# A graph network's second edge loop: penalty tables, paired outputs, and smaller macros at the end

## The chip, the cores and the metric

The kernel runs on one core of a Trainium2 chip. Its time is the device time of one execution in microseconds; the figure for a kernel is the median of its runs. One further execution is taken with the hardware profiler, and all views below come from that one. PE is the matrix engine (PEld its weight loads), DVE the vector engine, ACT the scalar engine, POOL the engine that issues the gathers here, SP the engine that issues the plain DMAs.

## What is computed

6250 nodes with 128 features, 100,000 edges sorted by destination, 64 features an edge. Two layers, each added to its input and normalised:

```python
# layer 0: messages, mean over the edges of a destination
m = relu(x[src] @ W_ne[:128] + (edge_attr @ W_edge) @ W_ne[128:] + b_ne)
out = segment_sum(m, dst) / max(count, 1) + x @ W_self + b_self
x = layernorm(x + out)
# layer 1: attention with 4 heads of 32, every node also has a loop to itself
xl, xr = x @ w_l + b_l, x @ w_r + b_r
logits = (leaky_relu(xl[src] + xr[dst], 0.2) * att).sum(-1)
ex = exp(logits - segment_max(logits, dst)[dst])
out = segment_sum(xl[src] * ex / segment_sum(ex, dst)[dst], dst) + bias
out = (out - out.mean()) / (out.std() + 1e-5) * ln_w + ln_b
x = layernorm(x + out)
```

## The kernel before

The edges are cut into 784 tiles of 128, four tiles a group: 196 groups of 512 edges. For every tile POOL issues one indirect DMA that gathers 128 rows of 128 features by source (`gather`, L251) into a ring of 30 group slots. The program first makes the node tables; then it has two loops over the 196 groups, written as steps in which every engine's instructions stand in a fixed order (a manual schedule):

- the first edge loop (layer 0; pool `e0`), gathers from `xw_t`;
- the second edge loop (layer 1; pool `e1`), gathers from `xl_t`;
- a short end (`n2`) for the normalisation over all nodes.

In step `s` of the second loop, the gather of group `s+4` is issued, SP stores the sums of the step before and loads rows for a later group (`load_rows`: a window of `xr_t` into `xr` and the destinations into `ds`), and then:

- `both` (L668, L670): PE adds the turned gathered rows and the destinations' rows in PSUM, group `s`;
- `copy_both` (ACT, L674) and `leaky` (DVE, L677) for group `s-1`; `logits` (PE, L696) for `s-2`;
- `onehot_t` (ACT, L661 and L662) for `s+1`;
- `sums` of the groups due in this step: four products (L825), and a last product (L831) with the row carried over from the group before, which DVE scales (`old`, L829). `keep_sums` copies the result (`win`, L836), and SP stores it to `out_t` at a row that it first loads from `fst` into a register (`store_sums`, L839);
- `values` (DVE, L816) and `onehot` (DVE, L454) for the groups due in the next step;
- whatever is planned for this step: the stages of a macro, and outputs.

A macro is the set of groups whose segment maxima are found together: 4 heads x 12 groups are 48 rows of 512 logits. Its ten stages, one per step, are `m_logits` (ACT copies the logits; DVE makes the penalties `pen`, which are -1e30 where the destination changes, L716 and L717), `m_forward` and `m_back` (a running maximum in each direction on DVE, L721 and L725), `m_ends` (PE turns the rows' ends, L736), `m_groups` (DVE, a scan over the groups), `m_before` (PE, L757), `m_maxima` (DVE; the penalty of the first segment `fp` at L766, the maxima at L768; then Exp on ACT), `m_weights` (DVE scales an identity, `dg`, L791; PE turns the weights, L780 and L795), `m_left` (DVE copies `cb`, L800; PE turns the rest) and `m_ready` (ACT). Groups of a macro can be summed from two steps after its last stage. There are 17 macros: fifteen of 12 groups, one of 9, one of 7.

```python
when, busy = {}, {}
begin = []
for k, m in enumerate(MS):
    begin.append(max(m.g0 + m.mg + 2, begin[k - 1] + 6 if k else 0))
    ...
    for u in range(m.g0, m.g0 + m.mg):
        s = max(begin[k] + len(M_STEPS) + 1, when.get(u - 1, 0))
        while busy.get(s, 0) >= (1 if s < GN - 30 else 2):
            s += 1
```

So sums go one a step, and two a step from step 166 on. A block of 128 nodes is finished when its last group is summed: `out_load` reads it from `out_t`, `out_weights` three steps later and `output` one more step later compute on DVE (L852 to L875, and L246 to L248). There are 49 blocks, of which the last two come together at the very end. Steps 0 to 195 take up a group each; the last step is 218.

Of the kernel before, what the change touches and what calls it, by code (L numbers as in the profile page):

```python
# [9 lines left out]
F32 = mybir.dt.float32  # L10
# [3 lines left out]
OP = mybir.AluOpType  # L14
# [3 lines left out]
P = 128  # L18
N = 6250
E = 100000  # L20
D = 128
DE = 64
H, C = 4, 32
SLOPE = 0.2
EPS = 1e-5
NB = -(-N // P)
# [28 lines left out]
RAW = 12  # L55
MACROS = (12,) * 15 + (9, 7)
AHEAD = 4
# [18 lines left out]
def gnn_resnorm(  # L76
# [353 lines left out]
    def near():  # L430
        ctx = ExitStack()
        with ctx:
            keep = ctx.enter_context(tc.tile_pool(name="near", bufs=1))
            sum_t = dram.tile([NR, W0], F32, name="sum_t")
            xr_t = dram.tile([NR, D], F32, name="xr_t")
            out_t = dram.tile([NR, H * HV], F32, name="out_t")
            kps = ctx.enter_context(tc.tile_pool(name="nearp", bufs=1, space=PSUM))
            rows_q = kps.tile([P, W + D], F32, name="rows_q")
# [7 lines left out]
            for t, n in ((sum_t, W0), (out_t, H * HV)):  # L446
                nc.scalar.dma_start(t[NP - P:NP, :], zero[:, 0:n])
                nc.scalar.dma_start(t[NP:NR, :], zero[:, 0:n])
            nc.scalar.dma_start(xr_t[NP:NR, :], zero[:, 0:D])

            def onehot(pool, g, dtype):
# [183 lines left out]
            with tc.tile_pool(name="e1", bufs=3) as pool, tc.tile_pool(name="e1m", bufs=2) as mp, \  # L635
# [14 lines left out]
                XR, DS, PZ, Z, OH, V, PA, WIN, OUTS = {}, {}, {}, {}, {}, {}, {}, {}, {}  # L650

                def load_rows(g):
                    XR[g] = pool.tile([W, D], F32, name="xr", bufs=9)
                    nc.sync.dma_start(XR[g], xr_t[bass.ds(first_row(g), W), :])
                    DS[g] = pool.tile([W, S], F32, name="ds", bufs=9)
                    nc.sync.dma_start(DS[g], bass.AP(tensor=dpad.tensor, offset=dpad.offset + 1 + g * S,
                                                     ap=[[0, W], [1, S]]))
# [14 lines left out]
                def copy_both(g):  # L672
                    Z[g] = pool.tile([P, S], F32, name="z")
                    nc.scalar.copy(Z[g], PZ[g])  # L674
# [27 lines left out]
                def m_load(m):  # L702
                    m.dm = mp.tile([m.R, S + 2], F32, name="dm")
                    for h in range(H):
                        nc.sync.dma_start(m.dm[h * m.mg:(h + 1) * m.mg, :],
                                          bass.AP(tensor=dpad.tensor, offset=dpad.offset + m.g0 * S,
                                                  ap=[[S, m.mg], [1, S + 2]]))

                def m_logits(m):
                    m.lg = mp.tile([m.R, S], F32, name="lg")
                    nc.scalar.copy(m.lg, m.plg)

                    m.pen = mp.tile([m.R, S + 1], F32, name="pen")
                    nc.vector.tensor_tensor(m.pen, m.dm[:, 1:], m.dm[:, 0:S + 1], op=OP.not_equal)  # L716
                    nc.vector.tensor_scalar(m.pen, m.pen, -BIG, None, op0=OP.mult)  # L717

# [4 lines left out]
                def m_back(m):  # L723
                    m.sm = mp.tile([m.R, S], F32, name="sm", bufs=1)
                    nc.vector.tensor_tensor_scan(m.sm[:, ::-1], m.pen[:, S:0:-1], m.fw[:, ::-1], -BIG,  # L725
                                                 op0=OP.add, op1=OP.max)

                    m.ends = mp.tile([m.R, 2], F32, name="ends")
                    nc.vector.tensor_scalar(m.ends[:, 0:1], m.dm[:, S:S + 1], m.dm[:, 0:1], -BIG,
                                            op0=OP.not_equal, op1=OP.mult)  # L730
                    nc.vector.tensor_copy(m.ends[:, 1:2], m.fw[:, S - 1:S])

                def m_ends(m):
                    m.pe = ps1.tile([P, S], F32, name="pw")
                    for i in range(2):
                        nc.tensor.transpose(m.pe[0:1, i * P:i * P + m.R], m.ends[:, i:i + 1], ident[0:m.R, 0:m.R])  # L736

# [22 lines left out]
                def m_maxima(m):  # L760
                    R = m.R
                    prev = mp.tile([R, 1], F32, name="prev")
                    nc.vector.tensor_copy(prev, m.pv[0:R, 0:1])

                    fp = mp.tile([R, S], F32, name="fp", bufs=1)
                    nc.vector.tensor_scalar(fp, m.dm[:, 1:S + 1], m.dm[:, 0:1], -BIG, op0=OP.not_equal, op1=OP.mult)  # L766
                    m.mx = mp.tile([R, S], F32, name="mx")
                    nc.vector.scalar_tensor_tensor(m.mx, fp, prev, m.sm, op0=OP.add, op1=OP.max)  # L768
# [65 lines left out]
                def keep_sums(u):  # L834
                    WIN[u] = pool.tile([W, H * HV], F32, name="win", bufs=4)
                    nc.scalar.copy(WIN[u], PA[u])  # L836

                def store_sums(u):
                    nc.sync.dma_start(out_t[bass.ds(first_row(u), W), :], WIN.pop(u))  # L839

# [48 lines left out]
                when, busy = {}, {}  # L889
                begin = []  # L890
                for k, m in enumerate(MS):
# [14 lines left out]
                stop = max(when.values())  # L906
                for b in range(NB - last):
                    s = when[FINAL[b]] + 1
                    for i, f in ((1, out_load), (4, out_weights), (5, output)):
                        plan(s + i, f, b, 1)  # L910
                    stop = max(stop, s + 5)
                stop += 1
# [9 lines left out]
                for s in range(stop + 1):  # L922
# [355 lines left out]
```

## Time and profile before

| | us |
|---|---|
| median of 3 runs | 2864.68 (2855.61 to 2869.66) |
| the profiled execution | 2204.19 |
| its span, first to last instruction | 2202.5 |
| mean granted TensorE clock | 0.83 |
| first gather from `xw_t`, last gather from `xw_t` issued | 83, 1000 |
| first gather from `xl_t`, last gather from `xl_t` issued | 1037, 2040 |
| PE, DVE, ACT, POOL busy | 1576, 1306, 715, 1508 |

The runs without the profiler are 660 us longer than the profiled execution. Busy shares are means over stages that have different limits; a stretch of the trace, or a single step, tells more. A row of the slices is 55 us wide, and a digit is the busy share in tenths.

### The profile page before, as it was taken

The numbers are of one execution on the slowest core, as the hardware profiler recorded it, in microseconds if no ns is written. First come the engines' busy times: TensorE is split into PE (matmuls) and PEld (weight loads), VectorE is DVE, ScalarE is ACT, GpSimd is POOL, SyncE is SP. The second block draws the span as 40 slices with busy tenths as digits, with TensorE's granted clock in tenths as the row PEclk, the third lists the DMA queues.
The fourth block names the chain that finished last, engine by engine and source line by source line (L and its number), as shares of the span: only waits on it lengthen the run. The fifth ranks groups of instructions, "written<-read, shape, count | busy, mean of one in ns | idle before, by whom it ended". The sixth has DMA issues, their size and how long they took to land.

```text
span 2202.5 us, 27258 instructions
## 1 busy us (share of the span) xinstructions
PE 1576.4 (72%) x6577; PEld 884.7 (40%) x6577; DVE 1306.1 (59%) x3710; ACT 715.0 (32%) x1724; POOL 1508.2 (68%) x1574
## 2 busy tenths in 40 slices
PE   4796566656666666674778888888888888889660
PEld 2574444444444444442223333333434344434440
DVE  4584445555666667775124455555556666677776
ACT  1341111111122112221344444444444444445214
POOL 7577777777777777772777777777777777777000
PEclk7897777777777787775779999999999999988755
DMA  5554444444444444432433444444444444443011
GB/s 148 143 119 96 95 95 95 93 99 99 99 98 103 105 103 101 106 90 80 119 101 105 112 113 115 114 113 111 112 113 116 115 113 119 111 115 101 24 26 59
DMA packets 292634, 225.37 MB, mean 102 GB/s; under 512 B 143289, under 2 KB 247591, under 8 KB 292466
## 3 DMA queue, kind: packets, MB, share of 16 engines
q1 hardware_dynamic: 241200, 120.47, 20.5%
q0 software_dynamic: 50048, 102.60, 19.9%
q8 instruction: 56, 0.92, 0.2%
q14 instruction: 112, 0.92, 0.1%
q10 hardware_dynamic: 1218, 0.47, 0.1%
HBM read 189.85 MB, written 33.52 MB: 101 GB/s over the span
## 4 chain that ended last, share of the span: by engine, by line
DMA 27%; DVE 19%; PE 18%; POOL 17%; issue 17%; ACT 2%; DVEq 0%; POOLq 0%; ACTq 0%; SPq 0%
POOL ring L251 17%; DMA ring<-xl_t,src_i 14%; DMA ring<-xw_t,src_i 10%; PE plg L696 4%; PE pz L670 4%; PE pa L825 3%; DVE a L454 3%; PE pz L668 2%; DVE msg L528 2%; DVE v L816 1%; PE pa L831 1%; DMA ring<-in_x_dram,src_i 1%; DVE win L542 1%; PE bank L194 1%; DVE ln_st L135 1%
## 5 line engine op out<-in xcount | busy, mean ns | idle before, releaser
L251 POOL DMA_INDIRECT ring<-xl_t,src_i x782 | 765.0, 978 | 274.4 <-issue 105.5
L251 POOL DMA_INDIRECT ring<-xw_t,src_i x734 | 693.3, 945 | 238.0 <-issue 195.6
L677 DVE SCALAR_TENSOR_TENSOR z<-z,pz 128x512 f32<-128x512 f32 x196 | 134.3, 685 | 377.4 <-ACT z L674 377.1
L519 DVE TENSOR_TENSOR ph<-ph,ring 128x512 f32<-128x512 f32 x184 | 128.6, 699 | 316.4 <-DMA ring<-xw_t,src_i 280.9
L668 PE MATMUL pz<-ident,ring 128*128 128x128 f32 x784 | 186.1, 317 | 146.9 <-DMA ring<-xl_t,src_i 140.5
L510 PE MATMUL ph<-wc,fT 128*128 128x256 f32 x784 | 288.2, 504 | 0.0
L524 ACT ACTIVATE msg<-ph 128x512 fp32r<-128x512 f32 x196 | 117.3, 599 | 524.1 <-DVE ph L519 471.2
L825 PEld LDWEIGHTS pa<-v,a 128*96 128x96 f32 x1568 | 201.2, 175 | 159.2 <-issue 107.0
L825 PE MATMUL pa<-v,a 128*96 128x136 f32 x1568 | 248.5, 305 | 8.6 <-DVE a L454 5.2
L537 PE MATMUL pa<-win,sel 96*1 96x129 f32 x390 | 91.2, 324 | 223.6 <-DVE win L542 221.7
L696 PE MATMUL plg<-z,attw 128*48 128x512 f32 (+2 forms) x392 | 228.2, 667 | 0.0
L670 PE MATMUL pz<-ds,xr 96*128 96x512 f32 x392 | 220.2, 645 | 0.1
L454 DVE TENSOR_TENSOR a<-rows_q,dl 128x384 fp32r<-128x384 f32 (+1 forms) x392 | 214.3, 547 | 0.0
L510 PEld LDWEIGHTS ph<-wc,fT 128*128 128x128 f32 x784 | 184.5, 254 | 61.1 <-issue 32.0
L836 ACT COPY win<-pa 96x136 f32<-96x136 f32 x196 | 52.5, 268 | 478.8 <-PE pa L831 460.9
L668 PEld LDWEIGHTS pz<-ident,ring 128*128 128x128 f32 x784 | 95.5, 146 | 258.7 <-DMA ring<-xl_t,src_i 185.1
L535 PE MATMUL pa<-msg,a 128*96 128x258 f32 x784 | 178.8, 362 | 0.0
L661 ACT ACTIVATE ds<-ds,nb 96x512 f32<-96x512 f32 x196 | 142.1, 725 | 8.4 <-DMA xr<-xr_t 8.4
L662 ACT ACTIVATE ds<-ds,ones 96x512 f32<-96x512 f32 x196 | 141.5, 722 | 6.4
L528 DVE SCALAR_TENSOR_TENSOR msg<-ph,msg 128x512 fp32r<-128x512 f32 x196 | 135.5, 691 | 0.9 <-ACT msg L524 0.8
L674 ACT COPY z<-pz 128x512 f32<-128x512 f32 x196 | 113.5, 579 | 69.6 <-PE pz L670 69.6
L535 PEld LDWEIGHTS pa<-msg,a 128*96 128x96 f32 x784 | 133.2, 210 | 1.0 <-PE pa L535 0.4
(198 smaller groups left out, 1798.5 us busy)
## 6 DMA issues: line engine op xcount, KB each, us to landing
ds<-dpad SPq DMA_DIRECT2D x196, 192.0 KB
ef<-in_edge_attr_dram SPq DMA_DIRECT2D x48, 512.0 KB
ring<-xl_t,src_i POOLq DMA_INDIRECT x782
ring<-xw_t,src_i POOLq DMA_INDIRECT x734
out_t<-win SPq DMA_DIRECT2D x196, 51.0 KB
sum_t<-win SPq DMA_DIRECT2D x196, 48.4 KB
xr<-xr_t SPq DMA_DIRECT2D x196, 48.0 KB
s<-out_t SPq DMA_DIRECT2D x47, 68.0 KB
```

Of the source, the lines that this page charges most:

```text
L251: nc.gpsimd.indirect_dma_start(out=to, out_offset=None, in_=table[0:min(table.shape[0], NP), :], in_offset=bass.IndirectOffsetOnAxis(ap=in ...
L454: nc.vector.tensor_tensor(a, over(iota_q, G), spread(dl[:, g * G:(g + 1) * G], W), op=OP.is_equal)
L510: nc.tensor.matmul(ph[:, 2 * i:2 * i + 2, :], fT[:, i, :], wc, start=i == 0 or g >= RAW, stop=g >= RAW, skip_group_check=g < RAW)
L528: nc.vector.scalar_tensor_tensor(msg[:, :, 1, 0:D], PH.pop(g), 0.0, msg[:, :, 0, 0:D].bitcast(F32), op0=OP.max, op1=OP.subtract)
L535: nc.tensor.matmul(pa, a[:, j, :], msgs[g % 3][:, j], start=j == 0, stop=j == G - 1)
L661: nc.scalar.activation(DS[g], DS[g], AF.Abs, bias=nb[0:W, g:g + 1])
L662: nc.scalar.activation(DS[g], DS[g], AF.Relu, bias=ones[0:W, 0:1], scale=-1.0)
L668: nc.tensor.matmul(pz[:, j * P:(j + 1) * P], XG[g][:, j, :], ident, is_transpose=True, start=j == 0, stop=False, skip_group_check=True)
L670: nc.tensor.matmul(pz, XR.pop(g), DS.pop(g), start=False, stop=True, skip_group_check=True)
L677: nc.vector.scalar_tensor_tensor(Z[g], Z[g], SLOPE, PZ.pop(g), op0=OP.mult, op1=OP.max)
L696: nc.tensor.matmul(m.plg, attw[m.mg][:, m.mg - i:m.mg - i + m.R], Z.pop(g), start=i == 0, stop=i == m.mg - 1)
L825: nc.tensor.matmul(pa, a[:, j, :], v[:, j].rearrange("p h c -> p (h c)"), start=j == 0, stop=j == G - 1)
```

## The change

Four things change in `near`.

1. Two tables in DRAM, `pen_t` (196 x 513) and `fp_t` (196 x 512), are made once, ahead of the first edge loop, from the padded destinations. A macro loads `pen` and `fp` from them, eight DMAs instead of four, and the five DVE instructions that made them and `ends` fall away.
2. Outputs take two blocks at once, but for the last of them.
3. The macros are fourteen of 12 groups, then 8, 6, 5, 4, 3 and 2. A macro of fewer than 12 groups takes two stages in each step (`pace`), and its sums go two a step.
4. The row number for a store is loaded in the step of the sums (`ROW`), one step ahead of the store. `xr` and `ds` have 6 buffers instead of 9 and are loaded 4 steps ahead instead of 7, `z` has 2 instead of 3, `win` 8 instead of 4.

```diff
-MACROS = (12,) * 15 + (9, 7)
+MACROS = (12,) * 14 + (8, 6, 5, 4, 3, 2)
...
+            with tc.tile_pool(name="ch", bufs=1) as pool:
+                HG = GN // 2
+                dm = pool.tile([HG, 2, S + 2], F32, name="dm")
+                for i in range(2):
+                    nc.sync.dma_start(dm[:, i, :], bass.AP(tensor=dpad.tensor, offset=dpad.offset + i * HG * S,
+                                                           ap=[[S, HG], [1, S + 2]]))
+                pen = pool.tile([HG, 2, S + 1], F32, name="pen")
+                nc.vector.tensor_tensor(pen, dm[:, :, 1:], dm[:, :, 0:S + 1], op=OP.not_equal)
+                nc.vector.tensor_scalar(pen, pen, -BIG, None, op0=OP.mult)
+                fp = pool.tile([HG, 2, S], F32, name="fp")
+                for i in range(2):
+                    nc.vector.tensor_scalar(fp[:, i, :], dm[:, i, 1:S + 1], dm[:, i, 0:1], -BIG,
+                                            op0=OP.not_equal, op1=OP.mult)
+                    nc.sync.dma_start(pen_t[i * HG:(i + 1) * HG, :], pen[:, i, :])
+                    nc.sync.dma_start(fp_t[i * HG:(i + 1) * HG, :], fp[:, i, :])
...
-                    XR[g] = pool.tile([W, D], F32, name="xr", bufs=9)
+                    XR[g] = pool.tile([W, D], F32, name="xr", bufs=6)
...
-                    DS[g] = pool.tile([W, S], F32, name="ds", bufs=9)
+                    DS[g] = pool.tile([W, S], F32, name="ds", bufs=6)
...
-                    Z[g] = pool.tile([P, S], F32, name="z")
+                    Z[g] = pool.tile([P, S], F32, name="z", bufs=2)
...
-                    m.dm = mp.tile([m.R, S + 2], F32, name="dm")
+                    m.pen = mp.tile([m.R, S + 1], F32, name="pen", bufs=3)
+                    m.fp = mp.tile([m.R, S], F32, name="fp", bufs=3)
                     for h in range(H):
-                        nc.sync.dma_start(m.dm[h * m.mg:(h + 1) * m.mg, :], ...)
+                        rows = slice(h * m.mg, (h + 1) * m.mg)
+                        nc.sync.dma_start(m.pen[rows, :], pen_t[m.g0:m.g0 + m.mg, :])
+                        nc.sync.dma_start(m.fp[rows, :], fp_t[m.g0:m.g0 + m.mg, :])
...
-                    m.pen = mp.tile([m.R, S + 1], F32, name="pen")
-                    nc.vector.tensor_tensor(m.pen, m.dm[:, 1:], m.dm[:, 0:S + 1], op=OP.not_equal)
-                    nc.vector.tensor_scalar(m.pen, m.pen, -BIG, None, op0=OP.mult)
...
-                    m.ends = mp.tile([m.R, 2], F32, name="ends")
-                    nc.vector.tensor_scalar(m.ends[:, 0:1], m.dm[:, S:S + 1], m.dm[:, 0:1], -BIG,
-                                            op0=OP.not_equal, op1=OP.mult)
-                    nc.vector.tensor_copy(m.ends[:, 1:2], m.fw[:, S - 1:S])
...
-                    for i in range(2):
-                        nc.tensor.transpose(m.pe[0:1, i * P:i * P + m.R], m.ends[:, i:i + 1], ident[0:m.R, 0:m.R])
+                    for i, t in enumerate((m.fp, m.fw)):
+                        nc.tensor.transpose(m.pe[0:1, i * P:i * P + m.R], t[:, S - 1:S], ident[0:m.R, 0:m.R])
...
-                    fp = mp.tile([R, S], F32, name="fp", bufs=1)
-                    nc.vector.tensor_scalar(fp, m.dm[:, 1:S + 1], m.dm[:, 0:1], -BIG, op0=OP.not_equal, op1=OP.mult)
...
-                    WIN[u] = pool.tile([W, H * HV], F32, name="win", bufs=4)
+                    WIN[u] = pool.tile([W, H * HV], F32, name="win", bufs=8)
...
-                    nc.sync.dma_start(out_t[bass.ds(first_row(u), W), :], WIN.pop(u))
+                    nc.sync.dma_start(out_t[bass.ds(ROW.pop(u), W), :], WIN.pop(u))
...
-                    begin.append(max(m.g0 + m.mg + 2, begin[k - 1] + 6 if k else 0))
-                    plan(max(m.g0 + 1, begin[k - 2] + 7 if k > 1 else 0), m_load, m)
+                    begin.append(max(m.g0 + m.mg + 2, done - 3 // pace))
+                    pace = 1 if m.mg == MG else 2
+                    plan(max(m.g0 + 1, begin[k - 3] + 7 if k > 2 else 0), m_load, m)
                     for i, f in enumerate(M_STEPS):
-                        plan(begin[k] + i, f, m)
+                        plan(begin[k] + i // pace, f, m)
+                    done = begin[k] + (len(M_STEPS) - 1) // pace
                     for u in range(m.g0, m.g0 + m.mg):
-                        s = max(begin[k] + len(M_STEPS) + 1, when.get(u - 1, 0))
-                        while busy.get(s, 0) >= (1 if s < GN - 30 else 2):
+                        s = max(done + 2, when.get(u - 1, 0))
+                        while busy.get(s, 0) >= (1 if m.mg == MG and s < GN - 30 else 2):
...
-                for b in range(NB - last):
-                    s = when[FINAL[b]] + 1
+                b = 0
+                while b < NB - last:
+                    n = 2 if b + 2 <= NB - last - 4 else 1
+                    s = when[FINAL[b + n - 1]] + 1
                     for i, f in ((1, out_load), (4, out_weights), (5, output)):
-                        plan(s + i, f, b, 1)
+                        plan(s + i, f, b, n)
...
-                early = 7
+                early = 4
...
                     for u in due.get(s, ()):
+                        ROW[u] = first_row(u)
                         sums(u)
                         keep_sums(u)
```

More of the change, by code (lines that the diff above doesn't have):

```diff
@@ L436, in near @@
             out_t = dram.tile([NR, H * HV], F32, name="out_t")
+            pen_t = dram.tile([GN, S + 1], F32, name="pen_t")
+            fp_t = dram.tile([GN, S], F32, name="fp_t")
             kps = ctx.enter_context(tc.tile_pool(name="nearp", bufs=1, space=PSUM))
@@ L649, in near @@
                         nc.vector.tensor_copy(attw[mg][hs, (h + 1) * mg:(h + 1) * mg + 1], att_c[hs])
-                XR, DS, PZ, Z, OH, V, PA, WIN, OUTS = {}, {}, {}, {}, {}, {}, {}, {}, {}
+                XR, DS, PZ, Z, OH, V, PA, WIN, OUTS, ROW = {}, {}, {}, {}, {}, {}, {}, {}, {}, {}
                 def load_rows(g):
-                    XR[g] = pool.tile([W, D], F32, name="xr", bufs=9)
+                    XR[g] = pool.tile([W, D], F32, name="xr", bufs=6)
                     nc.sync.dma_start(XR[g], xr_t[bass.ds(first_row(g), W), :])
-                    DS[g] = pool.tile([W, S], F32, name="ds", bufs=9)
+                    DS[g] = pool.tile([W, S], F32, name="ds", bufs=6)
                     nc.sync.dma_start(DS[g], bass.AP(tensor=dpad.tensor, offset=dpad.offset + 1 + g * S,
@@ L702, in m_load @@
                 def m_load(m):
-                    m.dm = mp.tile([m.R, S + 2], F32, name="dm")
+                    m.pen = mp.tile([m.R, S + 1], F32, name="pen", bufs=3)
+                    m.fp = mp.tile([m.R, S], F32, name="fp", bufs=3)
                     for h in range(H):
-                        nc.sync.dma_start(m.dm[h * m.mg:(h + 1) * m.mg, :],
-                                          bass.AP(tensor=dpad.tensor, offset=dpad.offset + m.g0 * S,
-                                                  ap=[[S, m.mg], [1, S + 2]]))
+                        rows = slice(h * m.mg, (h + 1) * m.mg)
+                        nc.sync.dma_start(m.pen[rows, :], pen_t[m.g0:m.g0 + m.mg, :])
+                        nc.sync.dma_start(m.fp[rows, :], fp_t[m.g0:m.g0 + m.mg, :])
                 def m_logits(m):
@@ L763, in m_maxima @@
                     nc.vector.tensor_copy(prev, m.pv[0:R, 0:1])
-                    fp = mp.tile([R, S], F32, name="fp", bufs=1)
-                    nc.vector.tensor_scalar(fp, m.dm[:, 1:S + 1], m.dm[:, 0:1], -BIG, op0=OP.not_equal, op1=OP.mult)
                     m.mx = mp.tile([R, S], F32, name="mx")
-                    nc.vector.scalar_tensor_tensor(m.mx, fp, prev, m.sm, op0=OP.add, op1=OP.max)
+                    nc.vector.scalar_tensor_tensor(m.mx, m.fp, prev, m.sm, op0=OP.add, op1=OP.max)
                     nc.vector.tensor_sub(m.lg, m.lg, m.mx)
@@ L890, in near @@
                 begin = []
+                pace, done = 1, 0
                 for k, m in enumerate(MS):
-                    begin.append(max(m.g0 + m.mg + 2, begin[k - 1] + 6 if k else 0))
-                    plan(max(m.g0 + 1, begin[k - 2] + 7 if k > 1 else 0), m_load, m)
+                    begin.append(max(m.g0 + m.mg + 2, done - 3 // pace))
+                    pace = 1 if m.mg == MG else 2
+                    plan(max(m.g0 + 1, begin[k - 3] + 7 if k > 2 else 0), m_load, m)
                     for i, f in enumerate(M_STEPS):
-                        plan(begin[k] + i, f, m)
+                        plan(begin[k] + i // pace, f, m)
+                    done = begin[k] + (len(M_STEPS) - 1) // pace
                     for u in range(m.g0, m.g0 + m.mg):
-                        s = max(begin[k] + len(M_STEPS) + 1, when.get(u - 1, 0))
-                        while busy.get(s, 0) >= (1 if s < GN - 30 else 2):
+                        s = max(done + 2, when.get(u - 1, 0))
+                        while busy.get(s, 0) >= (1 if m.mg == MG and s < GN - 30 else 2):
                             s += 1
@@ L906, in near @@
                 stop = max(when.values())
-                for b in range(NB - last):
-                    s = when[FINAL[b]] + 1
+                b = 0
+                while b < NB - last:
+                    n = 2 if b + 2 <= NB - last - 4 else 1
+                    s = when[FINAL[b + n - 1]] + 1
                     for i, f in ((1, out_load), (4, out_weights), (5, output)):
-                        plan(s + i, f, b, 1)
+                        plan(s + i, f, b, n)
                     stop = max(stop, s + 5)
+                    b += n
                 stop += 1
```

## The prediction, made before the changed kernel ran

> **What bounds the kernel now.** I read the page's slices first, then stretches of the trace, then single instructions in order of time. The rows of the slices that matter:
>
> ```profile
> DVE  4584445555666667775124455555556666677776
> POOL 7577777777777777772777777777777777777000
> PEclk7897777777777787775779999999999999988755
> ```
>
> POOL is flat at 7 until the last three slices, and then empty: nearly all the time is paced by POOL's gathers, and about 165 us at the end are not. The groups of instructions say what a gather costs:
>
> ```profile
> L251 POOL DMA_INDIRECT ring<-xl_t,src_i x782 | 765.0, 978 | 274.4 <-issue 105.5
> L251 POOL DMA_INDIRECT ring<-xw_t,src_i x734 | 693.3, 945 | 238.0 <-issue 195.6
> ```
>
> With 0.30 us of issue between them four gathers take 5.0 us in the first edge loop (83 to 1000 us) and 5.1 us in the second (1037 to 2040 us). A step of the second loop handles one group, so 196 steps are about 1000 us and then the tail drains. Busy times by stretch, the last three of them from step 166, from step 181, and from step 196 (the first without a gather or a new group):
>
> ```profile
> 1300.00:1400.00 100.00, 85.19 (x377) 39.24 (x376) 55.11 (x134) 46.91 (x108) 75.92 (x80) 1.00 0.43 115
> ...
> 1893.00:1980.00 87.00, 73.19 (x306) 34.58 (x306) 59.05 (x204) 38.91 (x93) 66.26 (x69) 0.90 0.42 114
> 1980.00:2058.00 78.00, 69.73 (x310) 34.44 (x310) 58.42 (x180) 35.27 (x88) 45.95 (x46) 0.89 0.30 80
> 2058.00:2153.00 95.00, 54.03 (x240) 37.41 (x240) 71.95 (x285) 14.23 (x64) 0.00 (x0) 0.60 0.09 24
> ```
>
> In the middle PE is at 85 of 100 us and DVE at 55, both under POOL. From step 181 PE is at 70 of 78. In the drain DVE leads, 72 of 95, and the granted clock is 0.60. A step with two sums, in order of time:
>
> ```profile
> 1993.25 0.66 PE L668 MATMUL pz<-ident,ring 128*128 128x128 f32 x4
> ...
> 1995.67 1.17 PE L825 MATMUL pa<-v,a 128*96 128x136 f32 x8
> ...
> 1996.77 0.39 PE L831 MATMUL pa<-old,sel 96*1 96x136 f32 x2
> 1997.09 0.94 PEld L825 LDWEIGHTS pa<-v,a 128*96 128x96 f32 x8 [0.24 <-issue]
> ...
> 1997.50 0.29 DVE L829 TENSOR_TENSOR old<-pa,cb 96x136 f32<-96x136 f32 x1 [0.93 <-ACT win L836]
> 1997.72 0.68 DVE L816 TENSOR_TENSOR v<-ring,wm 128x512 f32<-128x512 f32 x1
> ...
> 1998.52 0.66 PE L668 MATMUL pz<-ident,ring 128*128 128x128 f32 x4
> ...
> 1999.85 1.21 DVE L725 TENSOR_TENSOR_SCAN sm<-pen,fw 48x512 f32<-48x512 f32 x1
> ```
>
> PE repeats every 5.26 us. DVE can't do the second `old` (L829) before PE has done the first sum, 4.25 us into the step, and a macro's scan starts only at 6.6 us, when PE is already 1.3 us into the next step. That is free today because PE needs the scan's result a step later.
>
> **The change, part by part.** Sums are against the profiled execution (2204.2 us, a span of 2202.5).
>
> *Tables.* Per macro DVE loses L716, L717, L766, L729 and L731: 0.68 + 0.43 + 0.53 + 0.18 + 0.13 = 1.95 us, 33 us over 17 macros. Up to step 165 POOL hides it. What it can give there is quieter gathers: the 52 gathers that overlap one of the removed instructions are 7 us longer in sum than 940 ns each. The Trainium skill (SBUF — State Buffer, the part on the shared port pair) says that a VectorE instruction in a 2-port mode or with two SBUF inputs excludes GpSimd from the port for its whole length, which would make most of the 33 us gather time, up to 25 us at POOL's 76%. The row contradicts that size: 33 ns mean excess x 782 is 26 us for all of DVE's work, of which 7 overlap these. I take -3, between 0 and -7. Making the tables costs two loads, DVE work of about 3 us (1026 columns twice, 512 twice, at the rows' 0.43 to 0.68 us per 512) and four stores, before the first `ef` load on SP: about 10 us late. POOL's gathers from `xw_t` start at 83 us without it, 12 groups are already there, and the consumers take groups in 2.1 us against POOL's 5.0 until they wait for it at 162 us: they catch up some 30 us later. Ring slots would hold POOL only at group 30, at 173 us. Cost 0; 10 if that cover failed. The eight loads a macro instead of four are 0.4 us of SP each, 3 us in a step in which SP idles about as long; their target is used a macro later: 0 to 2, I take 0.
>
> *Pairs.* The last blocks show both sizes: one block takes 3.4 us of DVE (2147.01 to 2150.38), the two together 4.4 (2150.38 to 2154.82), so a pair saves 2.3 us. Before step 166 this hides under POOL. From 166 to 181 the other engines fall 10 us further behind POOL (87 us for 15 steps of 5.1), and DVE's load and SP's chain of store, landing, load are the likely reason; pairs and tables take 6 us of DVE there, the first steps of the 8-macro return some: -4.
>
> *Rows a turn ahead, buffers.* A row's load takes SP 0.27 us, and its registers 0.2 us. Two stores stand 2.4 us apart because the second waits for the first to land, so moving the load gains nothing there: 0. `xr`/`ds` are asked for 4 steps ahead instead of 7, about 15 us before use, a wide margin beside stores that let the next one go after 2.4 us: 0. `z` with two buffers waits for a matmul of the step before: 0.
>
> *Macros.* By the code's own arithmetic the last macros begin at steps 178, 184, 189, 193, 196, 199 instead of 170, 182, 191, 198; sums in pairs fill 14 of the 15 steps from 181 instead of 9, and the last step is 212, not 218. The small macros take two of the ten stages per step. That puts into one step `m_back` and `m_ends`, `m_groups` and `m_before`, `m_maxima` and `m_weights`: DVE work followed by PE work that needs it. In PE's order of the changed program these PE instructions stand behind the step's sums and ahead of the next step's four L668. So PE now waits for DVE at the end of the step. From the step above: DVE is free at 6.6 us; the scan ends at 7.8, PE's two transposes at 8.15, the next L668 at 8.4 instead of 5.26: +3.1. `m_groups` (1.05 of DVE) the same way: +3.0. `m_maxima`: 1.6 us of DVE, Exp 0.63 and 0.19 on ACT, `dg` 0.25, PE 0.3: the next step at 9.8, +4.5. `m_left` waits for `cb`: +2.2. First stage: 0. A macro costs 12.8 us of steps with two sums. In steps 181 to 195: 6.7 for the 8-macro's rest, twice 12.8, 3.0 for the 4-macro, and 3.1 where a pair's output stands ahead of the next `old` (step 189): 38.4. The steps themselves are 14 x 5.26 + 5 = 78.6 against the measured 78.0. So +39.
>
> The clock: PE would be about 73% busy here. The row with 84% has 0.90, the first loop with some 62% has 0.75, so about 0.82: +5 on 79 us of PE. The skill (TensorE: Matmul & The Clock Gate, Part 1) has a full idle window of 3.4 us throw the clock to half for at least as long; ten such waits would make +17. The rows interpolate, and I take +5 and keep 17 for the range.
>
> The drain, as a sum of DVE. Before: 20 `v` and `a` at 1.07, 22 `old` at 0.3, a hand-over of 1.0 in each of 10 steps with two sums, 3 + 8 for the macros, 12 blocks at 3.0 and the last at 4.8, 0.7 for L677: 91 us, plus waits, and 96.8 measured to 2154.8. After: 10 x 1.07, 12 x 0.3, 5 x 1.0, 2.6 + 6 + 6 for the macros, three pairs at 3.95, five blocks at 3.0, 4.8, 0.7: 66 us, with the same 6 of waits 72: -24.
>
> Sum: -3 - 4 + 39 + 5 - 24 = +13 us, profiled 2217. The median of the runs (2864.7) is 660 us, a factor 1.30, above the profiled execution, and no view shows why. Either gathers at 1.68 instead of 1.25 us, or half the granted clock in the second loop, would make it. I stretch +13 by 1.30 to +17: 2882.
>
> **Rivals.**
> Case A, above: PE and DVE in lockstep from 181, +17 (own range 0 to +50). For it: PE's order. Against it: the hidden waits are worked out from one kind of step.
> Case B, faster: the waits hide. If DVE reaches the macro's work before PE's sums end (old and `v` done earlier because the lag lets ACT and DVE run ahead), the stretch costs only its busy time, about +5, and the drain decides: -3 - 4 + 5 - 24 = -26, times 1.30 -34: 2831. It decides once the waits cost under 25 us in all, 2 us instead of 3 to 4.5 a stage. DVE's 0.93 us wait for ACT in the step above speaks against it, the 72 of 95 in the drain for it.
> Case C: in unprofiled runs gathers pace everything at 6.7 us a step. Then half of the 39 fits under them, the DVE savings too: -7, 2858. The steadiness of POOL speaks for it.
> Case D: the tables' loads or the shorter lead make `ds` late on SP: +60, 2925. The present trace has next to no PE wait for `xr` or `ds`.
> That the tables speed the long middle, as removed work suggests, is excluded by POOL's flat row.
>
> **How the numbers follow.** A 0.52, B 0.32, C 0.12, D 0.04. About 0.5%, 14 us, is what a measurement of this kernel can tell from no change. Slower by more: 0.40 of A's 0.52, and all of D: 0.44. Within: 0.12 of A, 0.02 of B, 0.08 of C, 0.22. Faster: 0.30 of B, 0.04 of C, 0.34. The range is 2822 to 2922: under it B's best, over it D and A with the clock's 17 and more.
>
> **What would show it.** Right: PE waits before the small macros' transposes and before `m_before`'s matmul, released by DVE's scan and copies, 3 us each; the group 195 taken up 20 to 40 us later after its gather than now; a drain of about 72 us from there; the gather mean near 970 ns. Wrong: the stretch from step 181 to 196 under 95 us (then B), a first loop that ends after 1005 us (the tables weren't hidden), DVE waits for `ds`.

## The result, and the profile after

| | before, us | changed, us | ratio |
|---|---|---|---|
| chip of the table above, 20 runs each | 2856.84 (2835.20 to 2875.52) | 2876.06 (2862.09 to 2893.53) | 1.0068 (1.0049 to 1.0086) |
| a second chip, 38 and 6 runs | 2206.55 (2200.32 to 2217.00) | 2225.42 (2222.10 to 2228.64) | 1.0089 (1.0070 to 1.0108) |

The changed kernel is slower by 19 us on both. The chips are of two sorts: that of the first row, and that of the first group of experiments, run the kernel before in about 2857 us, two others in 2207. The profile of before shown above (2204.2 us) is like the second sort; the first profile of the changed kernel, with a span of 2868.3 us, like the first. A second profile of the changed kernel comes from a chip of the second sort (span 2224.2 us), and steps are compared there. Medians are of all runs; a ratio leaves out those more than 1.5% above the fastest of their kernel, 8 of the 22 of `tables_later` below, so that its median and its ratio don't match.

The slices and the gathers of the changed kernel, on the faster chip:

```profile
DVE  4586455555666666775124444554555565666676
POOL 7577777777777777772777777777777777775000
PEclk7798778877777787775779999999999999988755
L251 POOL DMA_INDIRECT ring<-xl_t,src_i x782 | 764.5, 978 | 295.8 <-issue 79.6
L251 POOL DMA_INDIRECT ring<-xw_t,src_i x734 | 694.3, 946 | 240.3 <-issue 174.0
```

Up to the last four slices POOL's row is flat, as before, and a gather takes 978 and 946 ns, as before. In the last slice in which POOL works it has 5 and not 7: one of its last gathers waits 22 us for a ring slot, because the consumers are late. The two kernels by stretch, from the start of `leaky` of one group to that of another, and to the end of the last output (`leaky` of group 180 stands in step 181, so "180 to 195" is the prediction's stretch from step 181 to 196):

| us (faster chip) | before | changed | predicted difference | measured |
|---|---|---|---|---|
| group 0 to 165 | 846.1 | 846.5 | -3 | 0 |
| 165 to 180 | 86.5 | 80.6 | -4 | -6 |
| 180 to 195 | 78.0 | 125.9 | +44 | +48 |
| 195 to the last output | 96.8 | 73.6 | -24 | -23 |

The busy times of the changed kernel by stretch (columns as before: length, PE, PEld, DVE, ACT, POOL, granted clock, DMA share, GB/s); the last two are the stretch from 180 to 195 and the drain:

```profile
1300.00:1400.00 100.00, 85.62 (x379) 39.29 (x378) 50.30 (x111) 47.01 (x107) 75.65 (x80) 1.00 0.41 116
...
1976.80:2102.70 125.90, 98.77 (x438) 51.38 (x438) 74.81 (x206) 42.33 (x117) 49.18 (x51) 0.83 0.24 66
2102.70:2176.00 73.30, 37.64 (x161) 26.15 (x160) 55.05 (x210) 9.92 (x43) 0.00 (x0) 0.57 0.07 19
```

In the middle DVE has 50 us of work in 100 instead of 55, and the time is the same. From here on "the stretch" is that from 180 to 195. In it PE is busy 98.8 of 125.9 us (before 69.7 of 78) and the clock is 0.83 (before 0.89). In the drain DVE's 74 us (over all of its 96.8) have become 55. What PE waited for in the stretch (us in total, times, longest), first in the kernel before, then in the changed one:

```profile
PE pa L831 <- DVE old L829: 3.8, 2, 2.5
PE pw L795 <- DVE dg L791: 2.6, 1, 2.6
PE pz L668 <- DVE z L677: 1.2, 1, 1.2
PE pw L780 <- DVE cb L800: 0.9, 1, 0.9
```

```profile
PE pw L791 <- ACT lg L785: 10.8, 3, 3.6
PE pa L842 <- DVE old L840: 6.5, 2, 3.4
PE pw L791 <- DVE cb L811: 2.4, 2, 1.6
PE pw L770 <- DVE prev_r L766: 2.3, 1, 2.3
PE pw L770 <- DVE den L878: 2.2, 1, 2.2
PE pw L791 <- DVE m L863: 1.6, 1, 1.6
PE pw L770 <- DVE m L863: 1.0, 1, 1.0
```

`pw` is the PSUM tile of the macros' stages; where an output's line (`den`, `m`) is named as releaser, it is the DVE instruction just after the one that PE needs. PE stands for 27 us instead of 8. The 29 us by which it is busier are of two kinds. The stretch holds ten more sums (28 instead of 18: L836 has 224 records here, L825 144 in the kernel before), and a sum is 1.56 us of PE at full clock (1.17 + 0.39), so about 16 us are work that came from the drain. Most of the rest is the clock. Two macro steps in order of time, from the changed kernel's timeline (start, length, engine, line, and in brackets the idle time before and what ended it):

```profile
2018.51 0.39 PE L842 MATMUL pa<-old,sel 96*1 96x136 f32 x2
...
2020.85 0.16 DVE L766 COPY prev_r<-run 1x24 f32<-1x24 f32 x1
2021.15 0.18 PE L770 MATMUL pw<-ones,prev_r 1*24 1x1 f32 x2 [2.25 <-DVE prev_r L766]
2021.27 0.96 PE L688 MATMUL pz<-ident,ring 128*128 128x128 f32 x4
...
2022.02 1.92 PE L690 MATMUL pz<-ds,xr 96*128 96x512 f32 x2
2023.86 1.53 PE L716 MATMUL plg<-z,attw 128*20 128x512 f32 x2
...
2027.84 0.39 PE L842 MATMUL pa<-old,sel 96*1 96x136 f32 x2
...
2029.67 0.74 DVE L779 SCALAR_TENSOR_TENSOR mx<-fp,prev,sm 24x512 f32<-24x512 f32 x1
2030.44 0.68 DVE L781 TENSOR_TENSOR lg<-lg,mx 24x512 f32<-24x512 f32 x1
2031.16 0.63 ACT L785 ACTIVATE lg<-lg 24x512 f32<-24x512 f32 x1 [2.33 <-DVE lg L781]
2031.84 0.62 PE L791 MATMUL pw<-ident,lg 24*128 24x24 f32 x4 [3.61 <-ACT lg L785]
2032.81 1.11 PE L688 MATMUL pz<-ident,ring 128*128 128x128 f32 x4
2033.72 1.91 PE L690 MATMUL pz<-ds,xr 96*128 96x512 f32 x2
2035.56 1.90 PE L716 MATMUL plg<-z,attw 128*20 128x512 f32 x2
...
2042.43 0.40 PE L791 MATMUL pw<-ident,mx 24*128 24x24 f32 x4 [1.58 <-DVE m L863]
2042.76 0.66 PE L688 MATMUL pz<-ident,ring 128*128 128x128 f32 x4
2043.25 1.02 PE L690 MATMUL pz<-ds,xr 96*128 96x512 f32 x2
```

PE's next L688 stands at 2021.27, 2032.81 and 2042.76: steps of 11.5 and 10.0 us where two sums alone take 5.26. The waits of 2.25 and 3.61 us are paid twice: PE stands, and then L690 takes 1.92 and 1.91 us instead of 1.02, and L716 1.53 and 1.90 instead of 1.03, until the clock is granted again. The last wait shown, of 1.58 us, is paid once: L688 and L690 behind it take 0.66 and 1.02 us. What makes the difference is taken up under the clock, below.

### The profile page after: what moved, and what is told of

Same layout as the page of the kernel before. It is cut to its first block, busy times and chain, and to the rows that moved or that the text cites. A ratio compares the mean times of both kernels' runs of the same rounds, so it can differ in the third digit from the quotient of the medians.

```text
span 2868.3 us, 27096 instructions
## 1 busy us (share of the span) xinstructions
PE 1659.8 (58%) x6619; PEld 944.9 (33%) x6619; DVE 1261.2 (44%) x3424; ACT 723.6 (25%) x1718; POOL 1528.0 (53%) x1574
## 4 chain that ended last, share of the span: by engine, by line
PE 27%; another core or an unknown queue 25%; issue 18%; DVE 13%; POOL 10%; ACT 5%; DMA 2%; ACTq 0%; DVEq 0%; SPq 0%; POOLq 0%
POOL ring L251 10%; PE pa L836 6%; PE plg L716 5%; PE pz L690 5%; PE pz L688 3%; PE ph L530 2%; PE pa L842 2%; DVE a L474 2%; DVE msg L548 1%; PE pa L555 1%; ACT z L694 1%; ACT ds L681 1%; DVE win L562 1%; ACT win L847 1%
## 5 line engine op out<-in xcount | busy, mean ns | idle before, releaser
L251 POOL DMA_INDIRECT ring<-xl_t,src_i x782 | 784.0, 1003 | 636.6 <-issue 263.8
L836 PE MATMUL pa<-v,a 128*96 128x136 f32 x1568 | 283.7, 335 | 219.3 <-ACT v L823 116.7
L836 PEld LDWEIGHTS pa<-v,a 128*96 128x96 f32 x1568 | 231.9, 197 | 389.7 <-issue 179.5
L690 PE MATMUL pz<-ds,xr 96*128 96x512 f32 x392 | 246.6, 716 | 0.1
L847 ACT COPY win<-pa 96x136 f32<-96x136 f32 x196 | 52.6, 268 | 760.1 <-remote 386.4
L716 PE MATMUL plg<-z,attw 128*48 128x512 f32 (+5 forms) x392 | 238.2, 693 | 0.0
L688 PE MATMUL pz<-ident,ring 128*128 128x128 f32 x784 | 157.9, 331 | 129.3 <-issue 87.8
L562 DVE TENSOR_REDUCE win<-pa 96x129 f32<-96x258 f32 x196 | 81.9, 418 | 331.3 <-remote 268.4
L511 PE MATMUL pt<-ident,ef 128*128 128x128 f32 x392 | 101.9, 352 | 214.9 <-issue 95.4
L515 ACT COPY fT<-pt 128x256 f32<-128x256 f32 x196 | 72.7, 371 | 518.3 <-remote 321.9
L688 PEld LDWEIGHTS pz<-ident,ring 128*128 128x128 f32 x784 | 100.0, 163 | 192.7 <-issue 130.7
L511 PEld LDWEIGHTS pt<-ident,ef 128*128 128x128 f32 x392 | 60.9, 177 | 275.1 <-issue 141.6
```

The costliest lines, as they stand in the source:

```text
L251: nc.gpsimd.indirect_dma_start(out=to, out_offset=None, in_=table[0:min(table.shape[0], NP), :], in_offset=bass.IndirectOffsetOnAxis(ap=in ...
L511: nc.tensor.transpose(pt[:, g % 2, i, :], EF[c][:, o + 2 * i:o + 2 * i + 2, :], ident)
L688: nc.tensor.matmul(pz[:, j * P:(j + 1) * P], XG[g][:, j, :], ident, is_transpose=True, start=j == 0, stop=False, skip_group_check=True)
L690: nc.tensor.matmul(pz, XR.pop(g), DS.pop(g), start=False, stop=True, skip_group_check=True)
L716: nc.tensor.matmul(m.plg, attw[m.mg][:, m.mg - i:m.mg - i + m.R], Z.pop(g), start=i == 0, stop=i == m.mg - 1)
L836: nc.tensor.matmul(pa, a[:, j, :], v[:, j].rearrange("p h c -> p (h c)"), start=j == 0, stop=j == G - 1)
```

## The experiments

Ratios are against the kernel before on the same chip, with a 95% interval. `before_again`, `old_macros`, `new_macros` and `tables_later` ran together on a chip where before takes 2858.84 us; `shifted`, `tables_only`, `pairs_only` and `rows_only` on one where it takes 2206.74; the last four on a third, 2206.55.

**before_again: the kernel before, for a profile.** No edit.

> The kernel before, unchanged, for a profile that belongs to the time that its runs show: the profiled execution shown before took 2204 us while the runs took 2857. If the profile of the changed kernel (2868 us) shows the ordinary condition, this one will take 2840 to 2875 us, with POOL waiting for ring slots in both loops, gathers 5.9 us a group in the first loop and about 6.9 in the second, and the gathers from xw_t starting near 125 us; SP's first load of ef should then follow 2.5 us after the last store of xw_t, against 16.6 us in the changed kernel. If the two kernels really differ in this way, it takes about 2204 us again.

2856.42 us, span 2854.7. It belongs to its chip: the gathers from `xw_t` run from 124 to 1282 us (83 to 999 in the first profile of before, 125 to 1286 in the changed kernel's 2868.3 us). By stretch it gives the same picture as the faster chip: 180 to 195 takes 100.5 us, and 139.1 in the changed kernel; the drain 96.3 and 73.7. So it is the expectation's ordinary case, 2840 to 2875 us. What differs between the chips is taken up at the end.

**old_macros and new_macros: the change in two halves.** In the first the macros and their plan go back, in the second the kernel before gets them alone:

```diff
-MACROS = (12,) * 14 + (8, 6, 5, 4, 3, 2)
+MACROS = (12,) * 15 + (9, 7)
...
-    begin.append(max(m.g0 + m.mg + 2, done - 3 // pace))
+    begin.append(max(m.g0 + m.mg + 2, begin[k - 1] + 6 if k else 0))
...
-        plan(begin[k] + i // pace, f, m)
+        plan(begin[k] + i, f, m)
```

The second, against before, has the whole of the new plan and these two lines:

```diff
+m.dm = mp.tile([m.R, S + 2], F32, name="dm", bufs=3)
+Z[g] = pool.tile([P, S], F32, name="z", bufs=2)
```

> The changed kernel with fifteen macros of 12, one of 9 and one of 7, begun and loaded as before, one stage a step: what is left of the change is the tables, the outputs in pairs, and the rows a turn ahead with the smaller buffers. Theory 1 (the tables' loads and stores hold SP's first ef load back by 14 us at the start, and the first loop, which waits for its consumers and not for gathers, never gets it back): 2865 to 2875, slower than before by 10 to 15. Theory 2 (the prediction: the stages in pairs make PE wait for DVE at the end, and tables and pairs give 7): 2845 to 2857, not slower than before.

> The kernel before with the macros of 8 to 2 groups and their pace alone (dm with three buffers, and z with two, to make room). Theory 1 (start): 2852 to 2864, within 7 of before. Theory 2 (PE and DVE in lockstep from step 181: +39 and +5 for the stretch, -24 for the drain, stretched by 1.3): 2875 to 2885, slower by 20 or more.

Old macros: 2839.68 us, 0.9931 (0.9897 to 0.9964). New macros alone: 2897.23, 1.0122 (1.0078 to 1.0166). So the halves are -19 and +38, and their sum is the measured +19. Both lie on theory 2's side but outside its numbers, the first 5 us below, the second 12 above. Theory 1, which I had formed from the changed kernel's first profile (its first `ef` load stands 17 us behind the last store of `xw_t`), is out: with the tables still in place the kernel is faster than before. The new macros' kernel by stretch, 180 to 195 and from there to the last output:

```profile
2617.00:2773.00 156.00, 106.78 (x448) 54.27 (x446) 88.94 (x278) 42.91 (x121) 34.99 (x36) 0.79 0.15 41
2773.00:2851.00 78.00, 36.08 (x152) 24.81 (x152) 59.81 (x241) 10.42 (x46) 0.00 (x0) 0.55 0.07 19
```

156 us instead of 100.5, and 78 instead of 96.3: without pairs and tables the small macros cost still more in the stretch (55) and save less in the drain (18). One of PE's waits there is missing from the changed kernel's list:

```profile
PE pw L736 <- DVE ends L731: 5.0, 2, 2.6
```

**tables_later: the tables made behind the first two loads of `ef`.** The block that makes `pen_t` and `fp_t` moves, unchanged:

```diff
-with tc.tile_pool(name="ch", bufs=1) as pool:
-    HG = GN // 2
...
 for c in range(2):
     load_edges(c)
+with tc.tile_pool(name="ch", bufs=1) as chp:
+    HG = GN // 2
...
```

> The changed kernel with the block that makes the two tables moved behind the first two loads of ef, in a pool of its own beside those of the first loop, so that neither SP's order nor reused memory holds the ef loads back. Theory 1 (start): the first ef load stands 2 to 3 us after the last store of xw_t, and the time falls by 10 to 15 to 2861 to 2866. Theory 2 (the end): unchanged at 2871 to 2881.

2874.68 us, 1.0035 (1.0007 to 1.0063), against the changed kernel's 1.0068 (1.0049 to 1.0086), which was not measured beside it: the intervals overlap, so a gain of some 9 us is neither shown nor excluded by the times. Nor do the traces of the slower chip decide: the first `leaky` of the second loop starts at 1369 us here, 1377 in the changed kernel, 1375 in before, which has no tables to make, and 1359 in `old_macros`, which has them. The faster chip leaves little room for it (one profile each): there that instruction starts at 1049.7 us in the changed kernel, and at 1049.3 in `pairs_only` below, which makes no tables (1047.4 in the first profile of before).

**shifted: PE's stages a step behind DVE's.** The changed kernel with the ten stages of a small macro spread over six steps:

```diff
-plan(begin[k] + i // pace, f, m)
-done = begin[k] + (len(M_STEPS) - 1) // pace
+plan(begin[k] + (i if pace == 1 else (0, 1, 1, 2, 2, 3, 3, 4, 5, 5)[i]), f, m)
+done = begin[k] + (9 if pace == 1 else 5)
```

> The changed kernel with the stages of the small macros regrouped: forward and back in one step, then ends and groups, before and maxima, weights, and left with ready in a sixth step, so that no PE instruction needs DVE work of its own step but in the last of them. Lockstep theory (PE waits 2.3 to 3.6 us for prev_r, lg and the ends in each small macro, as the profile of the changed kernel shows): the stretch of steps 181 to 196 falls from 139 to 115 to 120 us, a step more of latency gives back 5, and the time is 2848 to 2862. Rival (the stretch is long because 14 of its 15 steps hold two sums, so that the waits only stand where DVE or PE would be busy anyway): 2870 to 2880.

2216.89 us, 1.0051 (1.0030 to 1.0072), on a chip where the changed kernel had not been run: by itself this decides nothing. So both were run together:

> The changed kernel, unchanged, beside its variants on one chip. One chip has run the kernel before in 2857 us and another in 2207. Lockstep theory on the 2207 chip: the sum of the prediction's profiled execution, 2217, with 117 us from the leaky of group 180 to that of group 195 (regrouped: 105; before: 78) and 56 to 60 from there to the last sum (before: 80); on the 2857 chip, 139 and 59 us and 2876 again. Rival (regrouping the stages changed nothing): the same stretch as the regrouped kernel within 3 us.

> The regrouped stages again, on the same chip as the changed kernel. Lockstep theory: faster than the changed kernel by 3 to 12 us. Rival (the sums in pairs fill the stretch): equal within 3.

The changed kernel 2225.42 us, 1.0089 (1.0070 to 1.0108), 8 us over what was expected of it, with a stretch of 125.9 where 117 was; regrouped 2211.31, 1.0026 (1.0011 to 1.0041), 14 us faster, 2 more than the most that was expected. The runs of the two don't overlap (2222.10 to 2228.64, and 2202.81 to 2219.51). The regrouped kernel's stretch, drain, and PE's waits in the stretch:

```profile
1982.00:2087.00 105.00, 85.19 (x416) 45.67 (x416) 72.76 (x200) 40.81 (x112) 48.31 (x49) 0.89 0.28 78
2087.00:2164.00 77.00, 38.26 (x174) 26.09 (x174) 57.43 (x214) 11.18 (x49) 0.00 (x0) 0.57 0.07 19
```

```profile
PE pa L842 <- DVE old L840: 11.2, 6, 3.1
PE plg L716 <- DVE z L697: 3.2, 1, 3.2
PE pw L806 <- DVE dg L802: 2.5, 2, 1.4
PE pw L791 <- DVE cb L811: 1.8, 2, 1.6
PE pw L791 <- DVE den L878: 1.6, 1, 1.6
```

The waits on `pw` fall from 20.3 to 5.9 us and PE's busy time from 98.8 to 85.2 (3 of it because the stretch holds 26 sums and not 28); the clock is back at 0.89. The waits for `old` grow by 5: of the six, two stand behind a macro's scan, two behind an output. There is also one of 3.2 us for `z`, and the drain grows by 4. So waits inside a step, with the clock that they cost, are what 18 of the stretch's 48 us were. A part stays: 105 us is still 27 more than before. About 12 of it are the eight more sums, about 11 PE's waits (19.8 instead of 8.3). So the rival, that the sums fill the stretch, has a share too.

**tables_only, pairs_only, rows_only: the other three parts, each alone on the kernel before.** The edits are items 1, 2 and 4 of the change (with the tables and with the rows, `z` has two buffers). Their expectations are in times of the slower chip; on the faster one only the differences compare.

> The kernel before with the two tables alone (z with two buffers, to make room). If the tables are what makes the kernel with the old macros 19 us faster than before (33 us of DVE work less over the second loop, which in these executions does not wait for gathers): 2838 to 2848. If that comes from the outputs in pairs, or the loads at the start cost 10 to 14 that nothing gives back: 2857 to 2870.

> The kernel before with the outputs in pairs alone. A pair saves 2.3 us of DVE, 21 pairs 48 us, and the drain has fewer outputs in it. If the outputs are what makes the kernel with the old macros faster: 2838 to 2848, with a drain (from the last group taken up to the last sum) of 70 to 75 us against 82. If the tables are: 2853 to 2860.

> The kernel before with the row numbers loaded a turn ahead, xr and ds with 6 buffers and asked for 4 steps ahead, z with two and win with eight. The prediction has 0 for this: 2852 to 2864. If SP's register load stood between two stores in the way of the next one (0.3 us a store, 196 of them, shown only where stores are late): up to 15 less. If the shorter lead makes ds late: 2870 or more.

| | us | ratio | 0 to 165 | 165 to 195 | drain |
|---|---|---|---|---|---|
| before | 2206.74 | | 846.1 | 164.5 | 96.8 |
| tables | 2204.28 | 0.9992 (0.9979 to 1.0004) | 851.9 | 160.3 | 93.2 |
| pairs | 2202.41 | 0.9980 (0.9970 to 0.9990) | 851.6 | 157.6 | 92.1 |
| rows, buffers | 2209.45 | 1.0009 (0.9997 to 1.0021) | 854.5 | 165.6 | 95.3 |

(The three columns at the right are from the profiles, the row of before from its first.) None comes near the 19 us that `old_macros` gained, and the gain of the tables alone is not clear of noise. By the profiles, tables and pairs take 8 and 12 us out of the steps from 165 on, where DVE counts. The times show less of it, and the profiles show where it went: the middle of the second loop is 5 to 8 us longer in each. There a gather takes 984 to 989 ns in the mean, and 978 in before: 6 to 11 ns on 782 gathers are 5 to 9 us.

**old_macros_b and last_paced: a version that beats both.**

The second differs from the first by:

```diff
-plan(begin[k] + i, f, m)
+plan(begin[k] + (i if k < len(MS) - 1 else (0, 1, 1, 2, 2, 3, 3, 4, 5, 5)[i]), f, m)
-s = max(begin[k] + len(M_STEPS) + 1, when.get(u - 1, 0))
+s = max(begin[k] + (11 if k < len(MS) - 1 else 7), when.get(u - 1, 0))
```

> Tables, outputs in pairs and rows ahead with the old macros again. From the parts measured one by one on the 2207 chip (tables -2, pairs -4, rows and buffers +3): 2203 there, 3 below before. On the 2857 chip 2840 again, 19 below before.

> The kernel with the old macros, tables, pairs and rows ahead, in which only the last macro, of 7 groups, takes its stages in six steps, regrouped, after the last group has been taken in. It then has its sums 4 steps earlier and the last step is 215 and not 218. Theory: where no new groups come in, PE is 40 of 72 us busy and has room for the waits: 3 to 8 below the kernel with the old macros. Rival (the drain is the sum of DVE's work, and that stays the same): within 2 of it.

The old macros with tables, pairs and rows ahead: 2193.60 us, 0.9945 (0.9925 to 0.9965), 13 below before, after 19 below on the slower chip. It is the best kernel of this study on both. With the last macro paced: 2198.41, 0.9966 (0.9952 to 0.9980), not the 3 to 8 us better of the theory; the 5 us by which it is worse are more than the rival's 2, but not clear of noise. The drain of each, old macros first:

```profile
2053.00:2143.00 90.00, 50.23 (x241) 34.93 (x240) 67.79 (x248) 13.81 (x61) 0.00 (x0) 0.66 0.10 26
```

```profile
2056.00:2148.00 92.00, 47.81 (x240) 33.14 (x240) 67.36 (x246) 13.61 (x61) 0.00 (x0) 0.66 0.10 25
```

Three steps fewer, the last sum 4 us earlier (68.8 instead of 73.1 us behind `leaky` of group 195), and the same 67 us of DVE in 92 and 90: the drain is paid in DVE work, not in steps, as the rival said. The expectation of `old_macros_b`, -3 from the sum of the parts, was short by 10. The profiles place that in the middle: each part alone has it 5 to 8 us longer than before, 20 in sum, and the three together have it as before (846.5 us, a gather mean of 976 ns). From 165 on the three together save 14.5 us, less than the 20 of the parts. Why gathers take 976 to 979 ns in some kernels and 984 to 989 in others was not settled.

## Why the prediction was right, and where it was not

The forecast was slower, 2882 against 2864.7, by PE and DVE in lockstep from step 181. It is slower, 2876.06 against 2856.84, and for that reason: the stretch is the one place that lost time (the table of stretches), the macros cost 38 us on the slower chip and 32 on the faster (2225.42 against 2193.60 of `old_macros_b`), and regrouping their stages gives 14 of the 19 back. By its steps:

*Tables at the start, 0.* The first `ef` load goes out at 97.7 us instead of 82.9, so 15 us late and not 10. The last gather from `xw_t` is issued at 1002 instead of 999. The cover held.

*Quieter gathers, -3.* It was 0: DVE does about 5 us less in every 100 of the middle, and a gather takes 978 ns as before. The Trainium skill (SBUF — State Buffer, the part on the shared port pair), as the prediction read it, would have made up to 25 us of it. The page limits its case of two SBUF inputs to GpSimd operations that read SBUF, and has whichever of the two starts first keep the pair, which the prediction left out. No run shows any of the 25.

*Pairs and tables from 166 to 180, -4.* Measured -6.

*Rows, leads and buffers, 0.* 1.0009 (0.9997 to 1.0021). In the stretch PE waits for no load of `xr` or `ds`, so case D, a late `ds`, is out.

*The waits, +38.4.* Of four kinds, one is not there. `m_ends` (L749) was to wait for the scan of `m_back`. But with the tables it turns the ends of `fp` and `fw`, and `fw` is made a step earlier; only in the kernel before does it take `ends`, which `m_back` writes. I took the order of the stages for a dependence and did not follow the operands in the diff. `new_macros`, which keeps `ends`, has this wait: twice, of up to 2.6 us (5.0 in all). The other three are there and somewhat shorter than worked out: `prev_r` 2.3 (3.0), `lg` 3.6 (4.5), `cb` 1.6 (2.2). The 3.1 for a pair's output ahead of `old` came as 3.0, and once more, behind the last group, as 3.4. In all PE's waits come to 27, 11 less than the sum; the two waits of 3.1 for the scan that are not there are 6 of that.

*The clock, +5.* This term was mis-sized, though the clock itself was not: 0.82 was forecast, 0.83 measured. The 79 us of PE's work were built of steps of 5.26 us, and the step that they come from ran at a granted clock of 1.00 throughout. So the loss to add was the whole way from 1.00 to 0.82, some 20 us, and not 5. In the trace PE is busy at half clock for 40.6 us of the stretch (15.4 before), and a matmul then takes about 1.9 times as long (1.91 against 1.02 us): some 19 of the 98.8 us are lost so, and 80 are left, near the 79 put.

The loss comes behind waits. Matmuls of the step at 2032.81 took 1.11, 1.91, 1.90 and 1.72 us for L688, L690, L716 and the first L836, against 0.66, 1.02, 1.03 and 1.17 at full clock, 2.8 us after one wait of 3.6. The three steps behind waits of 3.6 us lose 1.8 to 2.8 us so, and the three behind the two waits of 2.2 to 2.3 and the first of 1.6 some 1.7 each: 12 in these six. Most of the rest falls on the first step of the stretch, which starts at half clock, and on its end.

How long a wait must be can be read from the clock's own record. The granted clock is 1.00 or 0.50, and it changes only at multiples of 3.41 us. Take the windows of that length that ran at full clock, from 1100 to 2150 us in the nine profiles of the faster chips. Half clock followed 92 of the 93 in which PE was busy for less than half of the time, and 4 of the 1992 in which it was busy for more than 0.7 of it. (Between the two both happen; the ends of matmuls are modelled.) The wait of 2.25 us leaves its window busy for 0.34, and half clock follows. The wait of 1.60 us up to 1995.71 lies within one window, busy for 0.55, and half clock follows too; that of 1.58 us up to 2042.43 is spread over two, busy for 0.67 and 0.86, and full clock follows. The Trainium skill (TensorE: Matmul & The Clock Gate, Part 1) has an idle window of about 3.4 us throw the clock to half for at least as long. Counted so it made +17 and was nearer. The length of the window agrees with the trace, but the window need not be idle throughout: waits of 1.6 and 2.25 us within one were enough.

27 and 98.8 make the 125.9; the prediction had 38.4 and 84, which makes 122. An excess of 11 in the waits and a lack of 15 in the clock nearly cancel, and the 122 is right partly by luck.

*The drain, -24 to 72.8 us.* 73.6 measured. The differences came as summed: DVE's work fell by 18 us (20 in the sum), its idle time by 5 (the five hand-overs). The levels did not: DVE has 74 and 55 us of work where the sum has 81 and 61, and idles 6 to 7 us more than put, which cancels. That the drain is paid in DVE's work and not in steps is what `last_paced` shows too.

*Times 1.30.* This step failed. The 660 us lie between two sorts of chip, and not between runs with and without the profiler: `before_again`, profiled on the slower sort, takes 2856.42 us. The difference between the kernels is 19 us on both sorts, so nothing of it stretches with the total. And the 660 us came neither from slower gathers nor from a clock at half speed in itself: on the slower chip a gather takes 948 and 1003 ns (946 and 978), so case C, gathers that pace the whole at 6.7 us a step, is out. Without the factor the sum is +13, 6 short of the 19, the clock's term above all. The factor made +17 of it, so it brought the number nearer by luck.

*Case B*, the waits hide: it asked for a stretch under 95 us, and it is 125.9. Why a shorter drain did not pay: the 24 us that it lost were DVE's, and ten sums, 16 us of PE, went to a stretch where PE was already busy 70 of 78 us. *Group 195* is taken up 40 us after its gather instead of 18, as forecast; that gather itself was issued late, and group 194 waits 57 instead of 15.

## What to carry to other kernels

Two stages of a chain in one step of an in-order schedule make one engine wait for the other inside the step, also where both have idle time over a whole step; put the consumer a step behind, and read from the operands, not from the order of the stages, which pairs depend on each other. Price a wait on PE twice where it leaves a window of the clock (3.41 us here) less than half busy: once as idle time and once as the slow matmuls that follow it. Charge a forecast clock from the clock at which the priced step was measured. Work taken out of a drain is worth only what the stretch that receives it has to spare on its own bound engine.

## What the chips showed that I had not expected

The slower chips stop. In the middle of the second loop PE issues the same number of instructions in 900 us that it issues in 700 on the faster one. The kernel before, first profile (faster) and `before_again` (slower):

```profile
1100.00:1800.00 700.00, 586.08 (x2464) 262.40 (x2464) 373.59 (x979) 321.22 (x726) 533.80 (x545) 0.96 0.42 111
```

```profile
1450.00:2350.00 900.00, 637.00 (x2456) 310.06 (x2456) 368.37 (x960) 324.02 (x728) 531.24 (x532) 0.79 0.30 86
```

DVE, ACT and POOL have the same work; PE is busy 51 us longer, at 0.79 of the clock. The rest is time in which nothing computes. Counted in the traces from 80 us on, stops longer than 1.5 us in which PE, DVE and ACT all stand still come to 28 and 71 us in the first profile of before, and to 155 and 696 us in `before_again`: 625 of the 652 us between the spans. The changed kernel has 26 and 70 us, and 140 and 679. One of them, in the changed kernel on the slower chip:

```profile
1996.68 0.39 PE L842 MATMUL pa<-old,sel 96*1 96x136 f32 x2
...
1997.00 0.66 PE L688 MATMUL pz<-ident,ring 128*128 128x128 f32 x4
...
1997.49 1.02 PE L690 MATMUL pz<-ds,xr 96*128 96x512 f32 x2
...
1998.45 1.06 PE L716 MATMUL plg<-z,attw 128*48 128x512 f32 x2
2006.33 0.27 ACT L847 COPY win<-pa 96x136 f32<-96x136 f32 x1 [10.97 <-remote]
...
2006.80 1.45 PE L836 MATMUL pa<-v,a 128*96 128x136 f32 x5 [7.29 <-ACT v L823]
```

ACT's copy L847 needs the product L842, whose record ends at 1997.1 by the modelled ends; ACT starts at 2006.33, released by no recorded instruction, and PE then waits for ACT. All 22 such stops between 1600 and 2100 us end with L847, a consumer of PE. It looks as if results of PE reach the other engines up to 9 us late there (and 7 to 21 us at the start of the first loop, where the matmuls of 147 to 150 us release DVE and ACT at 156.74, 160.92 and 171.42). Whether PE finishes late, or only tells of it late, or the waiting engine itself is held up, and why on some chips alone, was not tried. The groups of the page show it in one field: the idle time before these copies is put down to PE on the faster chip, and for its largest part to an unknown releaser (`remote`) on the slower. The changed kernel, first on the faster:

```profile
L847 ACT COPY win<-pa 96x136 f32<-96x136 f32 x196 | 52.6, 268 | 519.1 <-PE pa L842 505.1
```

```profile
L847 ACT COPY win<-pa 96x136 f32<-96x136 f32 x196 | 52.6, 268 | 760.1 <-remote 386.4
```

The granted clock of 0.73 instead of 0.84 is then more likely a result of these stops than their cause: around this one, which begins at 1999.5 us, it stays at 1.00 until 2002 us and is 0.50 from 2004.
